# Drain's tables and tokens one step earlier, routing put off by a call, and the next layer's keys and values in the last rounds

## The chip, the cores and the metric

The kernel runs on one core of one Trainium2 chip. The metric is the device time of one execution in microseconds (us). The time of the kernel before is the median of three runs; one further execution was recorded by the hardware profiler, and all lines of the profile come from that one. A core has five engines that run side by side, each with its own instruction order: TensorE (PE; its weight loads are shown as PEld), VectorE (DVE), ScalarE (ACT), GpSimd (POOL) and SyncE (SP, which here issues most transfers). They wait for each other by semaphores.

## The reference

The input is x, 8 sequences of 256 tokens of width 256, and a context of the same shape. Two layers, all in float32, follow each other; each is a gated cross-attention and a gated mixture of experts:

```
x = x + tanh(g_xattn[0]) * attention0(layernorm(x), ctx)     # 16 heads of 16
x = x + tanh(g_ffn[0])   * experts0(layernorm(x))            # 8 experts, the best 2 of each token
x = x + tanh(g_xattn[1]) * attention1(layernorm(x), ctx)     # 16 heads of 16
x = x + tanh(g_ffn[1])   * experts1(layernorm(x))            # 7 experts and a no-op, capacity 256
```

attention: q from layernorm(x), k and v from the context, softmax(q k / 4) v, then an output projection with bias. experts0: logits = x @ gate_w, the two largest, softmax over the two, and for each chosen expert gelu(x W1 + b1) W2 + b2, weighted. experts1: softmax over 8 logits, the top two keep their probabilities; each of the 7 real experts takes the first 256 tokens that chose it, relu(x W1) W2, weighted; tokens that chose the eighth get x times that probability.

## The kernel before, in words

attention(layer) is a software pipeline of steps (b, g), with b from -2 to 7 and g from 0 to 3: b is a batch (a sequence of 256 tokens) and g one of four groups of four heads. The function `step` (L838 to L909) emits one step. The order on TensorE, VectorE, ScalarE and GpSimd is the order in which `step` and its helpers emit instructions (`tc.manual_schedule`, L1070); SyncE's order is left to a scheduler. What is called a drain below is `last_rows` (L1019 to L1065), which follows the last step (7,3).

The parts of a step that matter here:

- `maxima(b+1, g)` (L656, L661): scores of the next batch, and on VectorE their maxima, which `shift` puts into a row of the queries.
- `catch_up` and `some_routing(most, steps)`: the first emits what is in a list of postponed VectorE work and DMAs (`todo`); the second takes up to `most` operations from the routing of finished batches, and stops after `steps` marks ("step") that the routing yields.
- `weigh(b, g)` (L688, L695): scores s of a group, and exponentials ex on ScalarE. `sums(b, g-1)` (L712): weighted sums av of the group before, from ex and the values.
- `divide(b)` at the end of a batch: reciprocals on VectorE, a copy winv on GpSimd (L739), then den and at (L747, L751) on VectorE.
- `output(b-1)` at g=2: the projection po (L761). `normed_rows(b-2)`: the normalised rows rw, on GpSimd (L314), and their DMAs to `normed` and, in layer 0, acc. `turned_rows` (rt, L790) transposes them and `logits` (pl, L802) makes the router's logits.
- `keys(layer, b)` and `values(layer, b)` (pk at L543, pv at L574): keys and values of a batch; they come from the context alone. Each is 8 matmuls, split in two halves around `weigh`. A DMA writes ones into a row of the keys (kT<-ones, L563).

Routing works on groups of batches (0 to 2, 3 and 4, 5, 6, 7). For each group a generator `assign` emits top2, the mask and its running count, two matmuls pp (L367, L368) that give each token its place, the row numbers and idx (L481), and then one indirect DMA of GpSimd for each 128 tokens and each of two choices (the puts, who<-tok,idx, L486), which write a token's number into the list `who` at its place.

In layer 0 the experts' work is a list of tiles of 256 rows, sorted by expert. A table says of each tile which expert it has and where its list begins. The first three tiles (NFIRST = 3) are taken from the first five batches (NKNOWN = 5), so that they can start before the routing is over. `find_firsts` (L913), called at step (7,2), finishes the routing known so far, computes the table (`tables_first`, L1153), and lets SyncE load the first tile's weights (w_in_tf, w_out_tf, b1f, b2f), the token lists (ixf, L1192) and the weights of the other two. In the drain, after `divide(7)`, `gather_firsts` (L934) gathers the tiles' rows by indirect DMA (xrf, L1200), and `work_firsts` works the tiles between the rest of the drain: tf (transposes, L958), hf, gelu, yf.

After layer 0's experts `next_keys` (L1383) computes keys and values of layer 1's b=0 and b=1. Layer 1 starts with loading x_sb from acc (L1081); its step (-1,3) holds keys and values of b=2.

Of the kernel before, what the change touches and what calls it, by code (L numbers as in the profile page):

```python
# [55 lines left out]
def flamingo_kernel(  # L56
# [301 lines left out]
    def count(t0, n, mask):  # L358
        for t in range(n):
            nc.vector.tensor_add(run[:, t0 + t + 1, :], run[:, t0 + t, :], mask[:, t, :])  # L360
            yield
        yield "step"
# [8 lines left out]
    def assign(layer, t0, n, psum, tanh=False):  # L371
# [12 lines left out]
        if layer == 0:  # L384
# [3 lines left out]
            e2 = one("e2")  # L388
            if tanh:
                nc.scalar.activation(e2, d, AF.Tanh, scale=0.5)  # L390
            else:
                nc.scalar.activation(e2, d, AF.Exp)
            mask = per("mask")
            nc.vector.tensor_add(mask, oh1, oh2)
            yield
            yield from count(t0, n, mask)
# [12 lines left out]
        else:  # L409
# [3 lines left out]
            yield  # L413
            nc.scalar.activation(ex, ex, AF.Exp)
            yield "step"
# [35 lines left out]
        if layer == 1:  # L451
            yield from count(t0, n, mask)
            pp = before(layer, t0, n, mask, psum)
            yield "step"
# [130 lines left out]
    def attention(layer):  # L585
# [3 lines left out]
        with ExitStack() as st:  # L589
# [237 lines left out]
            def some_routing(most, steps=99):  # L827

                while most > 0 and groups:
                    got = next(groups[0], "done")  # L830
                    most -= 1
                    if got == "done":
                        groups.pop(0)
                    elif got == "step":
                        steps -= 1
                        if steps == 0:
                            break
# [7 lines left out]
            def step(b, g):  # L845
# [8 lines left out]
                some_routing(9 if b < B - 1 else 18, 1 if b < B - 1 else 3)  # L854
                if g == 0 and 0 <= b - 1:
                    sums(b - 1, NG - 1)
                    divide(b - 1)
                if g > 0 and 0 <= b < B:
                    sums(b, g - 1)
# [9 lines left out]
                if g == 0 and first_new <= b + 2 < B:  # L869
                    work = keys(layer, b + 2, bank, todo)  # L870
# [24 lines left out]
                if 0 <= b < B:  # L895
# [17 lines left out]
            def find_firsts():  # L913
                while groups:
                    some_routing(99)
                pt = ps_s.tile([P, 2 * S], F32, tag="s", name="pfirst")
                tables_first(pt[:, 0:E])
                b1 = small.tile([P, NFIRST, NF], F32, tag="b1f", name="b1f", bufs=1)
                b2row = const.tile([P, NFIRST, D], F32, tag="zrow", name="b2f")
                where = [tile_of(j) for j in range(NFIRST)]  # L920
                known = list(puts[0])
                for j in range(NFIRST):
                    firsts.append(
                        [load_tile(where[j][0], f"f{j}", b1[:, j, :], b2row[:, j, :])]
                    )
                    if j == 0:
                        for i in range(NFIRST):
                            ix = small.tile(
                                [P, 2], I32, tag="ixf", name=f"ixf_{i}", bufs=NFIRST
                            )  # L930
                            load_tokens(0, where[i][1], ix, known)
                            ixs.append(ix)

            ixs = []  # L934

            def gather_firsts():
                for j, ix in enumerate(ixs):
                    xr = sbe.tile([P, 2, W], F32, tag="ex", name=f"xrf_{j}")
                    gather_rows(0, ix, xr, NKNOWN * S)
                    firsts[j] += [ix, xr]  # L940

            def weigh_firsts():
                for j, t in enumerate(firsts):
                    w = small.tile([P, 2], F32, tag="wf", name=f"wf_{j}", bufs=NFIRST)
                    row_weights(w, t[2], r8[:, j : j + 1])
                    t.append(w)

            def work_firsts():
# [5 lines left out]
                def turn(j):  # L954
                    pt = bank(f"tf_{j}")
                    for c in range(NC_):
                        for i in range(2):
                            nc.tensor.transpose(  # L958
                                pt[:, c, ds(i * P, P)], firsts[j][2][:, i, ds(c * P, P)], ident
# [7 lines left out]
                for j in range(NFIRST):  # L967
                    wa, wb, b1, _ = firsts[j][0]
# [22 lines left out]
                    w = firsts[j][3]  # L991
                    firsts[j].append(y)
# [11 lines left out]
            def add_firsts():  # L1004
                for j, ((_, _, _, b2row), ix, _, w, y) in enumerate(firsts):
                    base = sbe.tile([P, 2, D], F32, tag="ex", name=f"basef_{j}")
                    for i in range(2):
                        nc.gpsimd.tensor_scalar(
                            base[:, i, :], b2row, w[:, i : i + 1], None, ALU.mult
# [7 lines left out]
            def last_rows():  # L1017
# [50 lines left out]
            first_new = 3 if layer else 0  # L1068
# [168 lines left out]
    def run_experts(layer):  # L1237
# [9 lines left out]
        with ExitStack() as st:  # L1247
# [135 lines left out]
            def next_keys():  # L1383

                todo = []
                bank = lambda name: ps.tile([P, NC_, S], F32, tag="h", name=name, bufs=3)
                for b in range(2):
                    for work in (keys(1, b, bank, todo), values(1, b, bank)):
                        for _ in work:
                            pass  # L1390
                for f in todo:
                    f()

# [5 lines left out]
            with order():  # L1399
# [3 lines left out]
                if layer == 0:  # L1403
                    next_keys()
# [75 lines left out]
```

## Time and profile before

| | |
|---|---|
| time, median of 3 runs | 964.3 us (960.97 to 979.55) |
| profiled execution | 1003.87 us, span 1002.1 us, mean granted TensorE clock 0.881 |
| TensorE busy | 860.0 us, 86% of the span |
| VectorE, ScalarE, GpSimd busy | 434.7, 318.4, 306.2 us |
| layer 0: attention, drain with the first three tiles, other tiles | 0 to 265, to 342, to 571 us |
| next_keys and the start of layer 1 | 571 to 617 us |
| layer 1: attention, drain, experts | 617 to 825, to 882, to 993 us |

A line of a timeline reads: start and length in us, engine, line of the kernel, operation, output<-input, and a count; in brackets how long the engine stood idle before it and what ended that. A line of the windows reads: the stretch, for each of TensorE, its weight loads, VectorE, ScalarE and GpSimd the busy time and the number of instructions, then TensorE's granted clock (1.00 is full), the busy share of the DMA engines, and GB/s. In the page's second part the span is cut into 40 slices; a digit is a share in tenths. "issue" as what ended an idle time means that the profile shows nothing that the engine waited for.

### The profile page before, as it was taken

How to read it: one execution, taken by the hardware profiler on the slowest of the kernel's cores; microseconds unless marked ns; L12 is line 12 of the kernel's file. 1: busy time of each engine (PE TensorE's matmuls, PEld its weight loads, DVE VectorE, ACT ScalarE, POOL GpSimd, SP SyncE). 2: the span in 40 equal slices, each digit the busy share in tenths (PEclk: the TensorE clock that was granted, in tenths of full speed). 3: DMA queues.
4: the chain of work that ended last, by engine and by line, in shares of the span. 5: the costliest groups of instructions: out<-in, count | busy, mean ns of one | idle time of the engine just before them, and what ended most of it. 6: DMA issues, size and time to landing. Idle time of an engine off the chain costs nothing. (4 is left out here: it accounts for less than half of the span.)

```text
span 1002.1 us, 15457 instructions
## 1 busy us (share of the span) xinstructions
PE 860.0 (86%) x5742; PEld 635.9 (63%) x5742; DVE 434.7 (43%) x1342; ACT 318.4 (32%) x732; POOL 306.2 (31%) x313
## 2 busy tenths in 40 slices
PE   1889999997578999999999958999999984069994
PEld 1556666564267788888888835566665533058883
DVE  1457877675535021111111245477787536501110
ACT  1135555543222232222222123355544351111110
POOL 2011332144334654333333301122221242532432
PEclk9879999896778999999999967599998775579998
DMA  9214442011562858685976281000000011135520
GB/s 267 82 45 123 122 115 60 13 39 38 169 201 66 270 135 234 199 254 163 264 197 188 23 287 58 1 4 23 13 13 3 22 60 51 34 95 163 185 84 32
DMA packets 103438, 110.15 MB, mean 110 GB/s; under 512 B 21888, under 2 KB 91117, under 8 KB 103361
## 3 DMA queue, kind: packets, MB, share of 16 engines
q1 hardware_dynamic: 71360, 80.33, 25.2%
q0 software_dynamic: 11168, 18.32, 7.9%
q10 hardware_dynamic: 20832, 10.50, 3.9%
q8 instruction: 46, 0.75, 0.3%
q14 instruction: 32, 0.25, 0.1%
HBM read 80.21 MB, written 29.55 MB: 110 GB/s over the span
## 5 line engine op out<-in xcount | busy, mean ns | idle before, releaser
L661 DVE TENSOR_REDUCE nm<-s 128x2 f32<-128x512 f32 x256 | 158.9, 684 | 104.3 <-PE s L656 99.6
L695 ACT ACTIVATE ex<-s 128x512 f32<-128x512 f32 x256 | 132.4, 602 | 157.8 <-PE s L688 156.2
L1299 PE MATMUL h<-xg,w_in_t 128*128 128x256 f32 (+1 forms) x576 | 111.1, 351 | 5.0 <-issue 3.3
L1287 DVE COPY xg<-xgt 128x512 f32<-128x512 f32 (+1 forms) x25 | 15.9, 638 | 225.3 <-PE xgt L1283 207.5
L656 PE MATMUL s<-kT,qT 16*128 16x256 f32 x1024 | 108.5, 450 | 5.4 <-ACT ex L695 4.3
L1337 PE MATMUL y<-w_out_t,hT 128*128 128x256 f32 x496 | 111.8, 379 | 0.0
L1299 PEld LDWEIGHTS h<-xg,w_in_t 128*128 128x128 f32 x576 | 97.2, 190 | 17.0 <-issue 4.2
L1309 ACT ACTIVATE hT<-h,b_t 128x256 f32<-128x256 f32 (+1 forms) x144 | 55.1, 442 | 163.9 <-issue 105.9
L1337 PEld LDWEIGHTS y<-w_out_t,hT 128*128 128x128 f32 x496 | 92.9, 190 | 11.9
L712 PE MATMUL av<-ex,va 128*32 128x256 f32 x1024 | 94.0, 437 | 4.9 <-ACT ex L695 2.5
L656 PEld LDWEIGHTS s<-kT,qT 16*128 16x128 f32 x1024 | 69.8, 206 | 37.7 <-issue 10.8
L688 PE MATMUL s<-qT,kT 17*128 17x256 f32 x1024 | 88.4, 437 | 4.4 <-issue 2.7
L486 POOL DMA_INDIRECT who<-tok,idx x64 | 63.2, 987 | 82.8 <-DVE s L504 22.5
L314 POOL TENSOR_SCALAR xn<-x_sb,mv,rstd 128x256 f32<-128x256 f32 x24 | 29.2, 1224 | 186.8 <-DVE rstd L296 136.0
L688 PEld LDWEIGHTS s<-qT,kT 17*128 17x128 f32 x1024 | 55.1, 202 | 32.0 <-issue 26.6
L1200 POOL DMA_INDIRECT xr<-xn,ix x45 | 44.6, 991 | 96.3 <-DMA ix<-who 57.3
L1230 POOL DMA_INDIRECT acc<-ysb,ix x31 | 49.3, 1591 | 74.1 <-DVE ysb L1345 58.8
L712 PEld LDWEIGHTS av<-ex,va 128*32 128x32 f32 x1024 | 33.3, 118 | 52.3 <-issue 24.7
L739 POOL COPY winv<-inv 128x512 f32<-128x512 f32 x16 | 9.9, 621 | 165.5 <-DVE h L294 147.5
L1345 DVE SCALAR_TENSOR_TENSOR ysb<-y,w,base 128x256 f32<-128x256 f32 x45 | 20.0, 479 | 78.6 <-PE y L1337 65.3
L1299 PE MATMUL h<-xg,w_in_b 128*128 128x256 f32 x224 | 52.1, 393 | 1.7 <-DVE w L1224 0.9
L1337 PE MATMUL y<-w_out_b,hT 128*128 128x256 f32 x224 | 50.2, 379 | 0.0
(203 smaller groups left out, 1112.4 us busy)
## 6 DMA issues: line engine op xcount, KB each, us to landing
w_in_t<-in_w_dram SPq DMA_DIRECT2D x18, 1024.0 KB
w_out_t<-in_w_dram SPq DMA_DIRECT2D x18, 1024.0 KB
who<-nobody ACTq DMA_DIRECT2D x14, 512.0 KB
w_in_b<-in_wi_dram SPq DMA_DIRECT2D x7, 1024.0 KB
w_out_b<-in_wx_dram SPq DMA_DIRECT2D x7, 1024.0 KB
xn<-rw SPq DMA_DIRECT2D x16, 256.0 KB
w_in_tf<-in_w_dram SPq DMA_DIRECT2D x3, 1024.0 KB
w_out_tf<-in_w_dram SPq DMA_DIRECT2D x3, 1024.0 KB
```

What stands on the lines that cost most here:

```text
L314: eng.tensor_scalar(dst, x_sb[:, t, :], mv[:, t, 0:1], rstd[:, t : t + 1], ALU.subtract, ALU.mult)
L486: put = nc.gpsimd.indirect_dma_start(out=who[layer][:, :], out_offset=bass.IndirectOffsetOnAxis(ap=idx[:, k, t : t + 1], axis=0), in_=tok[ ...
L656: nc.tensor.matmul(ps[j][:, i, :], qT[r, u, c, ds(i * P, P)], kT[r, u, c, :], start=True, stop=True,)
L661: nc.vector.tensor_reduce(nms[b][:, :, 4 * g + j], ps[j], AX.X, ALU.max, negate=True)
L688: nc.tensor.matmul(ps[j][:, k, :], kT[r, u, c, ds(k * P, P)], qT[r, u, c, :], start=True, stop=True,)
L695: nc.scalar.activation(ex, ps[j], AF.Exp, scale=HD**-0.5)
L712: nc.tensor.matmul(pav[ds(32 * j, 32), u, :], va[:, k, 4 * c + j, ds(32 * u, 32)], exs[j][:, k, :], start=(k == 0), stop=(k == 1),)
L1200: nc.gpsimd.indirect_dma_start(out=xr[:, i, :], out_offset=None, in_=normed[layer][0:among, :], in_offset=bass.IndirectOffsetOnAxis(ap=ix[ ...
L1230: put = nc.gpsimd.indirect_dma_start(out=acc[:, :], out_offset=bass.IndirectOffsetOnAxis(ap=to, axis=0), in_=y, in_offset=None, compute_op ...
L1299: nc.tensor.matmul(ph[:, fi, :], wa[:, c, ds((m * f2 + fi) * P, P)], xg[:, c, 0 : n * P], start=(c == 0), stop=(c == NC_ - 1),)
L1309: nc.scalar.activation(hT[:, f, 0 : n * P], ph[:, fi, :], AF.Gelu, bias=b1[:, f : f + 1],).ins
L1337: nc.tensor.matmul(py[:, i, :], hT[:, f, ds(i * P, P)], wb[:, f, :], start=(f == 0), stop=(f == NF - 1),)
```

## The change

1. Marks that routing yields become "stop" where ScalarE or TensorE work of the routing comes next (after `count`, and around the exponential of layer 1); `some_routing` ends its call there, so that this work is emitted one call later. The small activation e2 comes after the count.
2. In the last round (b = 7) of both layers `some_routing` may take 30 operations and 9 marks instead of 18 and 3, and `weigh(7, g)` comes before `sums(7, g-1)` and not after it.
3. `find_firsts` is split. The table and the first tile's weights come at step (7,1), the token lists at (7,2), and the weights of tiles 1 and 2 after the first tile's gathers, in the drain.
4. Keys and values of layer 1's b=0 and b=1 are computed in layer 0's rounds 6 and 7 (keys at g=0, values at g=3), and `next_keys` is gone. Those of b=2 come in layer 1's steps (0,0) and (0,3) and no longer in (-1,3).

```diff
     def count(t0, n, mask):
...
-        yield "step"
+        yield "stop"
...
+            mask = per("mask")
+            nc.vector.tensor_add(mask, oh1, oh2)
+            yield
+            yield from count(t0, n, mask)
             if tanh:
                 nc.scalar.activation(e2, d, AF.Tanh, scale=0.5)
             else:
                 nc.scalar.activation(e2, d, AF.Exp)
-            mask = per("mask")
-            nc.vector.tensor_add(mask, oh1, oh2)
-            yield
-            yield from count(t0, n, mask)
             pp = before(layer, t0, n, mask, psum)
...
             nc.vector.tensor_tensor(ex, logits, wide(m1), ALU.subtract)
-            yield
+            yield "stop"
             nc.scalar.activation(ex, ex, AF.Exp)
-            yield "step"
+            yield "stop"
...
             pp = before(layer, t0, n, mask, psum)
-            yield "step"
+            yield "stop"
...
+                    elif got == "stop":
+                        break
                     elif got == "step":
...
-                some_routing(9 if b < B - 1 else 18, 1 if b < B - 1 else 3)
+                some_routing(9 if b < B - 1 else 30, 1 if b < B - 1 else 9)
                 if g == 0 and 0 <= b - 1:
                     sums(b - 1, NG - 1)
                     divide(b - 1)
+                if b == B - 1:
+                    weigh(b, g)
                 if g > 0 and 0 <= b < B:
                     sums(b, g - 1)
...
-                if g == 0 and first_new <= b + 2 < B:
-                    work = keys(layer, b + 2, bank, todo)
+                if g == 0 and first_new <= b + 2 < known:
+                    work = keys(layer + (b + 2) // B, (b + 2) % B, bank, todo)
...
-                if g == 3 and first_new <= b + 2 < B:
-                    work = values(layer, b + 2, bank)
-                if layer == 1 and b == -1 and g == 3:
-                    work = itertools.chain(
-                        keys(1, 2, bank, todo),
-                        values(1, 2, lambda name: ps_s.tile([P, 2, D], F32, tag="s", name=name)),
-                    )
+                if g == 3 and first_new <= b + 2 < known:
+                    work = values(layer + (b + 2) // B, (b + 2) % B, bank)
...
-                if 0 <= b < B:
+                if 0 <= b < B - 1:
                     weigh(b, g)
...
+                if layer == 0 and b == B - 1 and g == 1:
+                    find_firsts()
                 if layer == 0 and b == B - 1 and g == 2:
-                    find_firsts()
+                    assert not groups
+                    token_firsts()
...
             def find_firsts():
-                while groups:
-                    some_routing(99)
                 pt = ps_s.tile([P, 2 * S], F32, tag="s", name="pfirst")
                 tables_first(pt[:, 0:E])
...
+                where.extend(tile_of(j) for j in range(NFIRST))
+                load_first(0)
...
+            def load_first(j, gets=()):
+                b1 = small.tile([P, NF], F32, tag="b1f", name=f"b1f_{j}", bufs=NFIRST)
+                firsts.append(load_tile(where[j][0], f"f{j}", b1, b2fs[:, j, :], gets))
...
+            def token_firsts():
                 known = list(puts[0])
...
+                for i in range(NFIRST):
+                    ix = small.tile([P, 2], I32, tag="ixf", name=f"ixf_{i}", bufs=NFIRST)
+                    load_tokens(0, where[i][1], ix, known)
+                    ixs.append(ix)
...
             def gather_firsts():
                 for j, ix in enumerate(ixs):
                     xr = sbe.tile([P, 2, W], F32, tag="ex", name=f"xrf_{j}")
-                    gather_rows(0, ix, xr, NKNOWN * S)
-                    firsts[j] += [ix, xr]
+                    gets = gather_rows(0, ix, xr, NKNOWN * S)
+                    xrs.append(xr)
+                    if j == 0:
+                        for i in range(1, NFIRST):
+                            load_first(i, gets if i == 1 else ())
...
                 sums(B - 1, NG - 1)
                 divide(B - 1)
                 if layer == 0:
+                    gather_firsts()
+                    some_routing(1)
                     nc.scalar.preload_act_table(AF.Gelu)
-                    gather_firsts()
...
-            first_new = 3 if layer else 0
+            first_new, known = (2, B) if layer else (0, B + 2)
...
-            def next_keys():
...
-                if layer == 0:
-                    next_keys()
```

More of the change, by code (lines that the diff above doesn't have):

```diff
@@ L1 @@
-import itertools
 from contextlib import ExitStack
@@ L913, in find_firsts @@
             def find_firsts():
-                while groups:
-                    some_routing(99)
                 pt = ps_s.tile([P, 2 * S], F32, tag="s", name="pfirst")
                 tables_first(pt[:, 0:E])
-                b1 = small.tile([P, NFIRST, NF], F32, tag="b1f", name="b1f", bufs=1)
-                b2row = const.tile([P, NFIRST, D], F32, tag="zrow", name="b2f")
-                where = [tile_of(j) for j in range(NFIRST)]
-                known = list(puts[0])
[L922 to L934, printed above, removed]
+                where.extend(tile_of(j) for j in range(NFIRST))
[3 more added lines that the diff above has]
+                firsts.append(load_tile(where[j][0], f"f{j}", b1, b2fs[:, j, :], gets))
+            where = []
+            if layer == 0:
+                b2fs = const.tile([P, NFIRST, D], F32, tag="zrow", name="b2f")
+            def token_firsts():
+                known = list(puts[0])
+                for i in range(NFIRST):
+                    ix = small.tile([P, 2], I32, tag="ixf", name=f"ixf_{i}", bufs=NFIRST)
+                    load_tokens(0, where[i][1], ix, known)
+                    ixs.append(ix)
+            ixs, xrs, wfs, yfs = [], [], [], []
             def gather_firsts():
@@ L938, in gather_firsts @@
                     xr = sbe.tile([P, 2, W], F32, tag="ex", name=f"xrf_{j}")
-                    gather_rows(0, ix, xr, NKNOWN * S)
-                    firsts[j] += [ix, xr]
+                    gets = gather_rows(0, ix, xr, NKNOWN * S)
[3 more added lines that the diff above has]
+                            load_first(i, gets if i == 1 else ())
             def weigh_firsts():
-                for j, t in enumerate(firsts):
+                for j, xr in enumerate(xrs):
                     w = small.tile([P, 2], F32, tag="wf", name=f"wf_{j}", bufs=NFIRST)
-                    row_weights(w, t[2], r8[:, j : j + 1])
-                    t.append(w)
+                    row_weights(w, xr, r8[:, j : j + 1])
+                    wfs.append(w)
             def work_firsts():
@@ L958, in turn @@
                             nc.tensor.transpose(
-                                pt[:, c, ds(i * P, P)], firsts[j][2][:, i, ds(c * P, P)], ident
+                                pt[:, c, ds(i * P, P)], xrs[j][:, i, ds(c * P, P)], ident
                             )
@@ L967, in work_firsts @@
                 for j in range(NFIRST):
-                    wa, wb, b1, _ = firsts[j][0]
+                    wa, wb, b1, _ = firsts[j]
                     hT = []
@@ L990, in work_firsts @@
                     y = sbe.tile([P, 2, D], F32, tag="ex", name=f"ysbf_{j}")
-                    w = firsts[j][3]
-                    firsts[j].append(y)
+                    w = wfs[j]
+                    yfs.append(y)
                     for i in range(2):
@@ L1004, in add_firsts @@
             def add_firsts():
-                for j, ((_, _, _, b2row), ix, _, w, y) in enumerate(firsts):
+                for j, (ix, w, y) in enumerate(zip(ixs, wfs, yfs)):
                     base = sbe.tile([P, 2, D], F32, tag="ex", name=f"basef_{j}")
@@ L1008, in add_firsts @@
                         nc.gpsimd.tensor_scalar(
-                            base[:, i, :], b2row, w[:, i : i + 1], None, ALU.mult
+                            base[:, i, :], b2fs[:, j, :], w[:, i : i + 1], None, ALU.mult
                         )
@@ L1381, in chain @@
                 second(turns[-1], hT)
-            def next_keys():
[L1385 to L1392, printed above, removed]
             order = lambda: tc.manual_schedule(
```

## The prediction

> **What bounds the kernel now.** I read the page first, then TensorE's timeline around each place the diff touches, then the other queues there. Page, rows 1 and 2:
>
> ```profile
> PE 860.0 (86%) x5742; PEld 635.9 (63%) x5742; DVE 434.7 (43%) x1342; ACT 318.4 (32%) x732; POOL 306.2 (31%) x313
> PE   1889999997578999999999958999999984069994
> PEclk9879999896778999999999967599998775579998
> ```
>
> TensorE is the bound almost everywhere; a slice is 25 us. It is short of work in three places: slices 10 to 13 (the end of layer 0's attention), 23 (the border) and 32 to 35 (the end of layer 1's attention). The change touches all three. The first one, TensorE's timeline:
>
> ```profile
> 261.74 3.38 PE L712 MATMUL av<-ex,va 128*32 128x256 f32 x16 [0.33 <-ACT ex L695]
> 281.36 0.45 PE L958 MATMUL tf<-ident,xrf 128*128 128x128 f32 x1 [16.25 <-DMA xrf<-xn,ixf]
> ```
>
> After the last weighted sums TensorE stands still for 16.25 us, waiting for the first tile's gathered rows. What is behind that, in POOL's and SP's timelines:
>
> ```profile
> 258.36 0.98 POOL L486 DMA_INDIRECT who<-tok,idx  x1 [0.30 <-issue]
> 267.15 0.62 POOL L739 COPY winv<-inv 128x512 f32<-128x512 f32 x1 [7.81 <-DVE h L294]
> 274.98 1.02 POOL L1200 DMA_INDIRECT xrf<-xn,ixf  x1 [7.21 <-DMA ixf<-who]
> 276.31 0.96 POOL L1200 DMA_INDIRECT xrf<-xn,ixf  x1 [0.30 <-issue]
> ```
>
> ```profile
> 263.61 0.42 SPq L1212 DMA_DIRECT2D w_in_tf<-in_w_dram  x1
> 264.22 0.39 SPq L1216 DMA_DIRECT2D w_out_tf<-in_w_dram  x1
> ...
> 266.35 2.19 SPq L1192 DMA_DIRECT2D ixf<-who  x3
> ```
>
> The token list ixf is issued at 266.35, behind 2 MB of weights, and lands at about 274.9, 8.6 us later; POOL then issues two gathers, and their data lands at 281.3. The same kind of load in layer 1 (ix) takes 1.99 us. The weights cannot go earlier because tables_first ends on VectorE at 260.6.
>
> **Layer 0's last round.** (a) Tables go to (7,1) and tokens to (7,2), so weights and ixf both leave before the last sums. What is late next is POOL: its order puts winv(7) before the gathers, and winv(7) starts 2.1 us after the last sums end (265.1 to 267.15) and takes 0.62. Then two gathers (2.3) and their landing (2.2 to 2.5) follow, so the hole is 2.1 + 0.6 + 2.3 + 2.5 = 7.5, say 7.8, against 16.25: **-8.45**. SP carries the rest of the step forward too: table reads, w_in, w_out, b1f, b2f and three ixf; tiles 1 and 2 load only after tile 0's gathers.
>
> (b) Keys and values of layer 1's b=0,1 come into rounds 6 and 7. Their price is the rows where they stood:
>
> ```profile
> 570.91 1.89 PE L543 MATMUL pk<-ctx_sb,wk 128*128 128x256 f32 x8
> ...
> 586.90 1.09 PE L631 MATMUL pt<-ident,xn 128*128 128x128 f32 x4 [8.92 <-DMA x_sb<-acc]
> ```
>
> Start to start 1.73 (pv begins at 572.63, and so on), four of them 6.9 at full clock. At the round's own clock (0.75 in the windows row below) it is 6.9 / 0.75 = **+9.2**. ScalarE's and VectorE's copies of them lie beside it: those engines are busy 13.1 and 21.6 of 40 us.
>
> (c) Scores ahead of sums, and routing's parts put off by a call, remove waits that the timeline shows: 2.60 before pp (L367, waits for mask), 0.65 and 0.33 for ex, and gaps of 0.62, 0.23 and 0.35 that end on issue: **-4.8**. Eight puts stay on POOL, now ahead of gbo(7) (1.25); x_sb with gbo is needed only in the drain, so this costs nothing unless the puts last beyond the last sums.
>
> The clock decides the size of this part. The windows:
>
> ```profile
> 100.00:175.00 75.00, 75.00 (x775) 48.72 (x778) 60.33 (x150) 41.02 (x96) 23.68 (x22) 1.00 0.35 100
> 225.00:265.00 40.00, 33.36 (x212) 18.12 (x212) 21.58 (x91) 13.14 (x30) 17.90 (x18) 0.75 0.17 48
> 265.00:281.00 16.00, 0.12 (x1) 0.00 (x0) 4.10 (x12) 1.76 (x2) 5.42 (x6) 0.61 0.98 336
> 625.00:650.00 25.00, 25.00 (x159) 14.57 (x158) 10.87 (x24) 10.02 (x22) 4.27 (x4) 0.50 0.00 1
> ```
>
> (The second number is TensorE's busy time, the third from the end the clock, then DMA share.) The Trainium skill, "TensorE: Matmul & The Clock Gate", section "What's actually happening", says the array drops to half rate after an idle window of about 3.4 us and comes back after as long a busy one. By the rule the filled round has no such gap and runs at 1.00: keys cost 6.9, and of the 33.4 busy us a quarter goes, 8.3: 6.9 - 4.8 - 8.45 - 8.3 = -14.7. By the rows it stays at 0.75: 9.2 - 4.8 - 8.45 = -4.1. The last row speaks against the rule: fully busy for 25 us, still at 0.50. I stay nearer the rows: **-8**.
>
> A second rule speaks against (a): "DMA: Bandwidth & Descriptors", section "Issuing engines are not separate DMA queues", says that all DMAs end on the same 16 engines and interleave. The row at 265 to 281 agrees (0.98 busy, 336 GB/s, ixf 8.6 instead of 1.99 us). 2.1 MB at 336 GB/s are 6.2 us. If the first tile's weights leave at about 255 they are through at 261, and ixf, which waits for the last put, lands about 264; if they overlap fully ixf lands near 270, about when winv(7) lets POOL go. So between 0 and +2; taken 0.
>
> **The border.** next_keys cost 6.9 us of TensorE but was followed by 8.92 us of waiting for x_sb: hidden. The wait's cause in SP's order:
>
> ```profile
> 574.46 4.03 SPq L563 DMA_DIRECT2D kT<-ones  x2
> 580.42 4.12 SPq L1081 DMA_DIRECT2D x_sb<-acc  x8
> ```
>
> kT<-ones ends its issue at 578.49 and lands about 580.3; it moves away with the keys. Next late is the last add into acc: issued 574.79 + 1.56, landing about 579.05. So **-1.3**, not -6.9.
>
> **Layer 1's start.** pk_2 and pv_2 (608.55 and 610.28, 1.89 each) stood in the shadow of the 2.56 us wait at 608.33 and of a shift; they go to (0,0) and (0,3), where TensorE is full (625 to 650 row). In full shadow before: 2 x 1.73 / 0.50 = 6.9 at most, less the 1.9 that the wait did not cover, so +5; in no shadow 0. Taken **+1.5**, near full clock.
>
> **Layer 1's last round.** This is where the change can hurt. The same larger quota (30 operations, 9 steps instead of 18 and 3) runs here too, and in the built order POOL now issues all twelve who puts of the first group before winv(6) and rw_5. Before, six went ahead and six after:
>
> ```profile
> 803.11 0.63 POOL L739 COPY winv<-inv 128x512 f32<-128x512 f32 x1
> 803.71 2.75 POOL L314 TENSOR_SCALAR rw<-x_sb,mv,rstd 128x256 f32<-128x256 f32 x2
> 806.62 1.08 POOL L486 DMA_INDIRECT who<-tok,idx  x1 [0.17 <-issue]
> ```
>
> ```profile
> 812.93 1.12 PE L790 MATMUL rt<-ident,rw 128*128 128x128 f32 x4
> ```
>
> Puts start 1.28 apart. idx_0 now stands behind lg of pl_4, about 2 us later (797.3): 12 x 1.28 = 15.4, so they end at 812.7, winv at 813.3, rw_5 at 816.1 instead of 806.5. Behind winv wait den and at (VectorE, 0.71 + 0.84) and with them po; behind rw_5 waits rt_5, and behind rt_5 in TensorE's order po, weigh(7,3), sums(7,2), pl_5, pp_6 and sums(7,3). Scores ahead of sums take away ex waits of 3.4 up to here (0.41, 0.87, 0.64, 0.76, 0.36, 0.36), so TensorE is at rt_5 at 809.5 and stands 6.6 us. From rt_5 to the last sums' end was 825.1 - 812.93 = 12.2, less 1.2 of waits is 11: end 827.1, +2 in this profile. In an execution with the full clock the old end would be about 819 (from 800 on at the windows' 0.77 to 0.81 instead of 1.00), the new one 825: +6. In the drain, routing work that is gone from the front lets m_10 start at 842.4 instead of 843.8: -1.4. So +0.6 to +4.6; taken **+3.5**, since the runs, at 961 to 980, were all shorter than the profiled 1003.87.
>
> **Sum.** -8 - 1.3 + 1.5 + 3.5 = -4.3. The profiled execution took 1003.87 us (span 1002.1, clock 0.88), the median of the runs 964.3; it would go to about 999.6. The terms are stalls more than clocked work, so I carry the same difference to the median: **960.0 us**. Own range 951 to 969.
>
> **Rivals.**
> A, the clock comes back: both last rounds become gapless, layer 0 gives the rule's -14.7, and layer 1's puts hide behind TensorE (-1.4, and its ex waits gone, 3.4 and 0.67 and 0.73 after them): -14.7 - 1.3 + 1.5 - 6.2 = -20.7, **944**. For: 100 to 175 at 1.00 with TensorE full. Against: 625 to 650, and twelve puts that exceed what TensorE has to do.
>
> B, slower: POOL's twelve puts. Place: rw_5 and winv(6) ahead of rt_5. Price: rt_5 at 816.1, and after 6.6 us of standing the rest at 0.50 takes 16 and not 11, so 832 against 819: +13, -1.4 from the drain. With layer 0 by the rows (-4.1), -1.3 and +1.5: +7.7, **972**. It decides once the stall and its clock cost more than about 6 us. For: 840 to 882 lies at 0.50 after waits. Against: the wait is only as long as the puts outlast TensorE's work.
>
> C, the change does not do what it says: gathers still wait, behind winv(7) or late puts, and the hole is filled by keys that cost nothing where they were. With the hole at 12 instead of 7.8 layer 0 gives -3.8, and the rest stays (-1.3, +1.5, +3.5): -0.1, **964**. For: POOL's order, which has not changed there.
>
> **How the numbers follow.** Forecast 0.50, A 0.18, B 0.15, C 0.17. 2% is 19.3 us (945.0 and 983.6), about what a measurement of this kernel can tell from no change. Faster by more than that needs most of A: 0.12. Slower needs more than B's price: 0.05. Same: 0.83. The range takes in C, B's and A's near halves: 945 to 975.
>
> **What would show it.** Right: tf_0 waits about 8 us for xrf, with POOL's gathers directly behind winv(7); ixf lands in 2 to 3 us; no wait at pp; four pk/pv groups in rounds 6 and 7; after next_keys' place x_sb<-acc starts about 1.3 us sooner after the last add; in layer 1, twelve puts in a row and a wait of 5 to 8 us at rt_5 for rw. Wrong: rt_5 without a wait (then towards A), tf_0 still over 12 us late (C), or the stretch after rt_5 at 0.50 (B).

## The result, and the profile after

| | before | after |
|---|---|---|
| median (20 runs each) | 969.36 us (960.97 to 983.6) | 961.64 us (956.19 to 964.37) |
| ratio after to before | | 0.9923, 95% interval 0.9905 to 0.994 |
| span and mean granted clock of the profiled execution | 1002.1 us, 0.881 | 958.9 us, 0.899 |

The change made the kernel about 8 us faster, 0.8%. The prediction said 960.0 us from a median of 964.3, within 2% and slightly faster: a difference of -4.3 us, where -7.7 was measured. The time was right; that it came so near was luck in part, since the three runs of before that it started from had a median 5 us under that of the twenty, and since errors in its steps cancelled.

The profile of before that the prediction used came from an execution with long stretches at a reduced clock. So before was profiled a second time (below: "before, second profile", span 968.9 us, clock 0.905), and all comparisons of stages use that one. Rows 1 and 2 of the page of after:

```profile
PE 818.9 (85%) x5742; PEld 616.2 (64%) x5742; DVE 435.4 (45%) x1342; ACT 316.8 (33%) x732; POOL 306.0 (32%) x313
...
PE   2889999999599699999999858999999863089994
...
PEclk9799999999799989999999957999997755589997
```

The work is the same, with as many matmuls as before. The three low places of before are still there, the first one narrower, and the fourteenth slice (312 to 336 us, digit 6) is a new one; it comes back below. TensorE's timelines, cut at the same marks in both kernels, give the stages (us; pt are the transposes of a batch's rows, xgt those of an expert tile's rows):

| stage | before | after | difference |
|---|---|---|---|
| layer 0 attention, to the end of the last sums | 250.5 | 240.3 | -10.2 |
| hole, to tf_0 | 16.7 | 12.1 | -4.6 |
| drain with the first three tiles, to the first xgt | 56.0 | 54.3 | -1.7 |
| layer 0's other tiles, to the last y | 231.1 | 239.9 | **+8.8** |
| border, to layer 1's first pt (keys included before) | 15.7 | 13.1 | -2.6 |
| layer 1 attention, to the end of the last sums | 223.1 | 225.9 | +2.8 |
| layer 1 drain, to its first xgt | 56.9 | 54.6 | -2.3 |
| layer 1 experts | 118.9 | 118.6 | -0.3 |

They sum to -10 us in these two executions. Within attention, a round is the time from one batch's shift (pm, in `shift`) to the next. Of the first row, -4.7 us are the sixth batch's round, -3.0 the two rounds after it up to the last sums, and -2.6 the first steps, where nothing had changed yet: TensorE's clock at 52 to 60 us was 0.50 in before and 0.83 in after, and another kernel with the change was as slow there as before. Over all profiles the second shift, batch 0's, came between 46.6 and 55.0 us, so the start says nothing about the change.

**The hole.** TensorE's, POOL's and SP's timelines of after:

```profile
239.27 1.07 PE L711 MATMUL av<-ex,va 128*32 128x256 f32 x16
242.26 0.51 PE L367 MATMUL pp<-run,ones 128*128 128x16 f32 x2 [1.49 <-DVE run L359]
252.40 0.45 PE L961 MATMUL tf<-ident,xrf 128*128 128x128 f32 x1 [9.63 <-DMA xrf<-xn,ixf]
```

```profile
239.90 0.97 POOL L485 DMA_INDIRECT who<-tok,idx  x1 [0.30 <-issue]
240.87 1.30 POOL L888 TENSOR_TENSOR x_sb<-x_sb,gbo 128x512 f32<-128x512 f32 x1
243.80 0.61 POOL L738 COPY winv<-inv 128x512 f32<-128x512 f32 x1 [1.63 <-DVE inv L735]
248.95 1.02 POOL L1204 DMA_INDIRECT xrf<-xn,ixf  x1 [4.54 <-DMA ixf<-who]
```

```profile
237.22 0.42 SPq L1216 DMA_DIRECT2D w_in_tf<-in_w_dram  x1
237.84 0.39 SPq L1220 DMA_DIRECT2D w_out_tf<-in_w_dram  x1
...
245.84 2.19 SPq L1196 DMA_DIRECT2D ixf<-who  x3
```

winv(7) is done at 244.4, and POOL still waits 4.54 us: not winv but the token list is late. ixf is issued 5 us after the last put ended on POOL (240.87), since the program has it wait for the puts to land, and they land while the first tile's 2 MB of weights are on their way.

**Layer 1's last round.** POOL and TensorE of after:

```profile
767.03 0.97 POOL L485 DMA_INDIRECT who<-tok,idx  x1 [0.30 <-issue]
767.99 0.63 POOL L738 COPY winv<-inv 128x512 f32<-128x512 f32 x1
768.60 2.74 POOL L313 TENSOR_SCALAR rw<-x_sb,mv,rstd 128x256 f32<-128x256 f32 x2
```

```profile
769.87 0.48 PE L789 MATMUL rt<-ident,rw 128*128 128x128 f32 x1 [5.14 <-POOL rw L313]
771.39 0.90 PE L789 MATMUL rt<-ident,rw 128*128 128x128 f32 x3 [1.04 <-POOL rw L313]
```

Twelve puts run without a break from 752.83; then winv; then rw; TensorE stands 6.2 us at rt_5. The windows of after, cut before and behind this wait:

```profile
751.30:764.70 13.40, 12.33 (x98) 6.33 (x98) 3.71 (x22) 9.39 (x21) 9.12 (x10) 0.74 0.18 57
764.70:771.40 6.70, 0.51 (x6) 0.19 (x2) 2.67 (x4) 0.00 (x0) 6.09 (x7) 0.50 0.09 29
771.40:785.70 14.30, 12.99 (x71) 8.58 (x71) 8.51 (x35) 5.48 (x13) 1.17 (x1) 0.62 0.18 55
```

Behind the wait TensorE works at a clock of 0.62 up to the last sums.

**What paid for it.** 4.7 us in layer 0's attention and 6.2 in layer 1's, where the last round hides them, come from a place that the prediction did not look at: the sixth batch's round. In before (second profile), ScalarE and TensorE in layer 1:

```profile
725.27 0.24 ACT L414 ACTIVATE ex<-ex 128x48 f32<-128x48 f32 x1 [6.19 <-DVE ex L412]
725.42 2.04 ACT L695 ACTIVATE ex<-s 128x512 f32<-128x512 f32 x4
```

```profile
726.05 2.14 PE L656 MATMUL s<-kT,qT 16*128 16x256 f32 x12 [1.95 <-ACT ex L695]
728.12 1.93 PE L712 MATMUL av<-ex,va 128*32 128x256 f32 x16
```

Routing's exponential takes 0.24 us, but it stands on ScalarE ahead of the four exponentials of the scores and waits 6.19 us for VectorE. TensorE then stands 1.95 us, and its next groups run slowly: 12 matmuls of s take 2.14 us where 16 take 1.29 at full clock, and 16 of av 1.93 where they take 1.07. The granted clock was 1.00 up to the wait, 0.50 from 728 to 732 us, and 1.00 again from 734. In after the same exponential comes behind the scores' four, and nobody waits:

```profile
710.49 2.06 ACT L694 ACTIVATE ex<-s 128x512 f32<-128x512 f32 x4 [3.35 <-PE s L687]
712.42 0.86 ACT L548 ACTIVATE qT<-pq,bqk 128x256 f32<-128x256 f32 x2
713.35 0.24 ACT L413 ACTIVATE ex<-ex 128x48 f32<-128x48 f32 x1
```

From shift to shift this round took 29.9 us before and 23.7 after in layer 1 (-6.2), and 30.1 before and 25.4 after in layer 0 (-4.7).

**Where it was given back.** In layer 0's other tiles TensorE waits for the third tile's rows. TensorE's timeline of after, then POOL's:

```profile
333.46 0.45 PE L1287 MATMUL xgt<-ident,xr 128*128 128x128 f32 x1 [4.69 <-DMA xr<-xn,ix]
336.59 0.90 PE L1287 MATMUL xgt<-ident,xr 128*128 128x128 f32 x3 [2.69 <-DMA xr<-xn,ix]
```

```profile
320.42 1.63 POOL L1234 DMA_INDIRECT acc<-ysbf,ixf  x1 [6.41 <-issue]
...
330.49 1.02 POOL L1204 DMA_INDIRECT xr<-xn,ix  x1 [0.16 <-issue]
331.82 1.58 POOL L1234 DMA_INDIRECT acc<-ysbf,ixf  x1 [0.30 <-issue]
333.70 1.01 POOL L1204 DMA_INDIRECT xr<-xn,ix  x1 [0.30 <-issue]
```

Before (second profile) had one wait there, and its first gather of the third tile went out behind three adds:

```profile
346.58 0.55 PE L1283 MATMUL xgt<-ident,xr 128*128 128x128 f32 x3 [2.73 <-DMA xr<-xn,ix]
```

```profile
337.99 1.04 POOL L1200 DMA_INDIRECT xr<-xn,ix  x1 [0.16 <-issue]
```

POOL's order in this stage is left to the scheduler. In before the third tile's two gathers (xr) stood behind three and four adds of the first tiles into acc; in after they stand behind five and six. Every kernel that has part 1 of the change, that with part 1 alone too, had its gathers behind two more adds than before, unless an edit below moved them.

### The profile page after: what moved, and what is told of

Its sections match the earlier page's. It is cut to its first block, busy times and chain, and to the rows that moved or that the text cites. A ratio compares the mean times of both kernels' runs of the same rounds, so it can differ in the third digit from the quotient of the medians.

```text
span 958.9 us, 15454 instructions
## 1 busy us (share of the span) xinstructions
PE 818.9 (85%) x5742; PEld 616.2 (64%) x5742; DVE 435.4 (45%) x1342; ACT 316.8 (33%) x732; POOL 306.0 (32%) x313
## 5 line engine op out<-in xcount | busy, mean ns | idle before, releaser
L1341 PE MATMUL y<-w_out_t,hT 128*128 128x256 f32 x496 | 113.8, 384 | 0.0
L655 PE MATMUL s<-kT,qT 16*128 16x256 f32 x1024 | 98.0, 431 | 1.2 <-ACT qT L548 0.6
L687 PE MATMUL s<-qT,kT 17*128 17x256 f32 x1024 | 83.6, 416 | 2.8 <-DMA qT<-nmT 1.4
L655 PEld LDWEIGHTS s<-kT,qT 16*128 16x128 f32 x1024 | 63.3, 197 | 30.4 <-issue 10.4
L711 PE MATMUL av<-ex,va 128*32 128x256 f32 x1024 | 77.3, 415 | 1.1 <-DVE nat L725 1.1
L687 PEld LDWEIGHTS s<-qT,kT 17*128 17x128 f32 x1024 | 53.5, 192 | 27.1 <-issue 19.4
L711 PEld LDWEIGHTS av<-ex,va 128*32 128x32 f32 x1024 | 28.9, 114 | 36.4 <-issue 18.5
```

Of the source, the lines that this page charges most:

```text
L655: nc.tensor.matmul(ps[j][:, i, :], qT[r, u, c, ds(i * P, P)], kT[r, u, c, :], start=True, stop=True,)
L687: nc.tensor.matmul(ps[j][:, k, :], kT[r, u, c, ds(k * P, P)], qT[r, u, c, :], start=True, stop=True,)
L711: nc.tensor.matmul(pav[ds(32 * j, 32), u, :], va[:, k, 4 * c + j, ds(32 * u, 32)], exs[j][:, k, :], start=(k == 0), stop=(k == 1),)
L1341: nc.tensor.matmul(py[:, i, :], hT[:, f, ds(i * P, P)], wb[:, f, :], start=(f == 0), stop=(f == NF - 1),)
```

## The experiments

Every experiment starts from the changed kernel unless said otherwise; ratios are to the kernel before on the same chip (after: 0.9923). The runs were made in four sets, in which before had medians of 969.8, 976.8, 995.3 and 974.8 us (the second and third on the same chip), and after itself was not run in them. So ratios of different sets are compared only roughly, and stages of the profiles are compared first, with the ratio beside them.

**A second profile of before.** No edit.

> The kernel before once more, unchanged, for a profile at the ordinary clock. Expected: span about 960 to 968 us. The hole before tf_0 is the same 16 us whatever the clock (it is made of transfers). In layer 1, rt_5 is not waited for; if the prediction's estimate at full clock holds, layer 1's stretch from its first pt to its first expert transpose (xgt) is 3 to 5 us shorter than the changed kernel's; if the early routing pays in the drain what the puts cost, it is the same or longer.

Measured: 970.71 us, span 968.9. The hole is 16.73 us. Layer 1 from its first pt to its first xgt takes 280.0 us before and 280.5 after: the second case, not the first. That seemed to say that the puts cost nothing in the end; the next run says otherwise.

**Layer 1 at the old quota.**

```diff
-                some_routing(9 if b < B - 1 else 30, 1 if b < B - 1 else 9)
+                most, marks = (30, 9) if layer == 0 else (18, 3)
+                some_routing(9 if b < B - 1 else most, 1 if b < B - 1 else marks)
```

> The changed kernel with layer 1's last round at the old quota (18 operations, 3 marks), layer 0 as changed. Theory (twelve puts in a row hold winv and rw back): six puts go behind rw_5, the waits of 5.14 and 1.04 us at rt_5 go, and the kernel is 3 to 5 us faster than the changed one (about 0.995 of it). Rival (the drain gets back what the puts cost): the routing that is not done early comes behind the last sums on VectorE, the last chain of layer 1 is as late as before, and the time is the same within 1.5 us or longer.

Measured: 952.38 us, 0.9838 (0.9795 to 0.9881). POOL, TensorE and the windows:

```profile
757.02 0.63 POOL L738 COPY winv<-inv 128x512 f32<-128x512 f32 x1
757.62 2.74 POOL L313 TENSOR_SCALAR rw<-x_sb,mv,rstd 128x256 f32<-128x256 f32 x2
760.53 1.07 POOL L485 DMA_INDIRECT who<-tok,idx  x1 [0.17 <-issue]
```

```profile
759.28 1.07 PE L711 MATMUL av<-ex,va 128*32 128x256 f32 x16
760.28 0.69 PE L789 MATMUL rt<-ident,rw 128*128 128x128 f32 x4
```

```profile
760.30:770.40 10.10, 9.13 (x72) 5.78 (x68) 3.12 (x9) 8.17 (x18) 8.24 (x9) 0.76 0.42 139
```

rt_5 follows the sums without a wait. From the last shift to the last sums' end it is 19.8 us, against 34.4 in after and 25.0 in before: the quota alone costs 14.5 us there, and 6.4 come back in the drain (61.0 against 54.6 us); 8.1 remain. (Attention and drain are 9.6 us shorter in all, but 1.7 of that is the round before, which takes 28.8 us in after and 27.1 here, and 27.1 also in two kernels below that keep the large quota; so it is not the quota's.) The theory is confirmed in kind, at about twice the expected size.

The 14.5 us have two parts. rt_5 with all its rows starts 20.1 us after the last shift instead of 9.7: 10.4 us. From there to the last sums it is 14.3 us at a clock of 0.62 instead of 10.1 at 0.76, with one more pair of routing's matmuls (pp): 4.2 us. The wait of 6.2 us is less than the first part because TensorE, at 0.74, came late to rt_5 itself. In three kernels below that keep the twelve puts (keys back, table back, token lists first) TensorE ran at 1.00 up to rt_5 and waited longer; with keys and values back:

```profile
766.35 0.48 PE L789 MATMUL rt<-ident,rw 128*128 128x128 f32 x1 [6.96 <-POOL rw L313]
```

Yet the stretch from the last shift to the last sums was 34.3 to 34.4 us in all of them. So POOL's row of puts sets the time of rt_5, and the clock before it changed nothing.

**Layer 1 with the puts behind winv and rw, large quota kept.**

```diff
                 catch_up()
+                early = layer == 1 and b == B - 1 and g == 0
+                if early:
+                    sums(b - 1, NG - 1)
+                    divide(b - 1)
+                    normed_rows(b - 2, nc.gpsimd)
                 some_routing(9 if b < B - 1 else 30, 1 if b < B - 1 else 9)
```

> The changed kernel with layer 1's step (7,0) in another order: the last sums of b=6, winv and rw_5 come before the routing, so before the twelve puts on GpSimd; the large quota stays. Theory (it is the puts' place ahead of winv and rw that costs, not the early routing): no wait at rt_5, the stretch from the last shift to the last sums goes from 34 us back to about 20 to 22, the drain stays short, and the kernel is 8 to 12 us faster than the changed one, as fast as or faster than with the old quota (950 to 953). Rival (VectorE's burst of early routing delays tr, den and nat, and so TensorE, whatever GpSimd's order): the last round keeps 5 us or more of the 14, and the kernel is slower than with the old quota by 3 us or more.

Measured: 955.5 us, 0.9809 (0.9759 to 0.9858). rt_5 does not wait; from the last shift to the last sums it is 28.7 us instead of 34.4, with the drain still short (54.5). So the order is worth 5.7 of the 8.1 us that the quota costs with its drain. The edit sets it on every engine, not on POOL alone. The rival has the rest: the last round keeps 8.9 of the 14.5 us, where the theory had expected 20 to 22 us for the whole round. TensorE now waits 3.12 us for the scores' exponentials, which stand on ScalarE behind rows of x_sb that wait for VectorE, and 2.92 us at pp for the mask from VectorE.

```profile
757.62 2.56 PE L687 MATMUL s<-qT,kT 17*128 17x256 f32 x12 [3.12 <-ACT ex L694]
```

**Keys and values back behind layer 0's experts** (next_keys restored, known = B for layer 0; b=2 stays).

> The changed kernel with the keys and values of layer 1's b=0 and b=1 computed after layer 0's experts again; those of b=2 stay at (0,0) and (0,3). Theory (moved work costs in the last rounds 4 x 1.73 = 6.9 us of TensorE, and was hidden behind the wait for x_sb): layer 0's last sums come 6 to 7 us earlier, the border costs 1.3 to 2.7 us more, so 4 to 5 us faster than the changed kernel. Rival 1 (the keys fill stalls and keep the clock up): the last round is hardly shorter, and the kernel is 1 to 3 us slower. Rival 2 (the hole is bound by the puts' landing and not by TensorE): the last sums come earlier but tf_0 does not; then the time is 1.3 to 2.7 us longer.

Measured: 956.98 us, 0.9875 (0.9828 to 0.9922). Counted from the same shift at the start, the last sums come 6.1 us earlier; the hole is 1.8 us longer, the border 15.6 instead of 13.1, the other tiles 2.1 shorter. The first part of the theory holds: the keys cost nearly what their matmuls take, 6.1 us of 6.9, and nothing was to be had for them at the border beyond 2.5 us. The second rival has a part, since 1.8 us go back into the hole, where ixf again leaves 5 us after the last put. The 2.1 us of the other tiles were in no theory. By the stages moving the keys was a loss of about 4 us; the ratios of the whole times (0.9875 and 0.9923, with intervals that overlap) do not show it for sure.

**Table, weights and tokens back at (7,2).**

> The changed kernel with the table, the first tile's weights and the token lists at step (7,2) again, and the weights of tiles 1 and 2 issued behind the token lists as before. Theory (the early table is what shortens the hole): the wait before tf_0 goes from 9.6 us back to about 13 to 16 us, +4 to +6 us, ratio to the changed kernel about 1.005. Rival (the puts' landing bounds it and the table comes early enough in any case): the wait stays within 2 us of 9.6, and the time within 2 us.

Measured: 967.55 us, 0.9998 (0.9972 to 1.0024). Last sums to tf_0: 18.6 us instead of 12.1; every other stage is within 1.4 us. So part 3 of the change is worth 6.5 us; table, weights and token lists move together here, and what each of them gives was not separated.

```profile
260.02 0.45 PE L959 MATMUL tf<-ident,xrf 128*128 128x128 f32 x1 [13.87 <-DMA xrf<-xn,ixf]
```

**Token lists ahead of the first tile's weights.**

```diff
-                load_first(0)
 ...
-                    load_tokens(0, where[i][1], ix, known)
+                    gots.append(load_tokens(0, where[i][1], ix, known))
                     ixs.append(ix)
+                load_first(0, gots)
```

> The changed kernel with the first tile's weights behind the token lists (waiting for them) and not ahead of them. Theory (the 2 MB of weights, at 237 to 244 us, hold up the landing of the last puts and of ixf): ixf is issued 2 to 3 us earlier and lands in about 2 us instead of 3, tf_0 comes 3 to 4 us earlier after the last sums, and the kernel is 2 to 4 us faster. Rival (the weights are then late): tf_0 comes earlier but the first hf waits for w_in, time equal or longer.

Measured: 963.85 us, 0.9892 (0.9843 to 0.9942). SP and TensorE:

```profile
242.00 2.19 SPq L1197 DMA_DIRECT2D ixf<-who  x3
...
245.93 0.40 SPq L1218 DMA_DIRECT2D w_in_tf<-in_w_dram  x1
```

```profile
249.04 0.44 PE L962 MATMUL tf<-ident,xrf 128*128 128x128 f32 x1 [6.81 <-DMA xrf<-xn,ixf]
252.95 0.90 PE L962 MATMUL tf<-ident,xrf 128*128 128x128 f32 x3 [3.47 <-DMA xrf<-xn,ixf]
```

With no weights in flight ixf is issued 1.6 us after the last put's end instead of 5.0, and the hole is 9.1 us: the weights did hold up the puts. But now the weights travel beside the gathers, whose second half comes 3.47 us later, and the drain is 3.2 us longer. Nothing is gained.

**Part 1 alone, on the kernel before** (the marks "stop" and the place of e2).

> The kernel before with the first part of the change alone (routing's ScalarE and TensorE parts put off by a call); quotas, tables, scores and keys as before. Theory (in the fifth round routing's small exponential stood on ScalarE ahead of the scores' four, and waited 6.2 us for VectorE; TensorE then stood about 1.9 us and ran at half clock for a while, once in each layer): the sixth shift comes about 6 us earlier after the fifth in layer 0 and in layer 1. The build also gives GpSimd the changed kernel's order of gathers behind layer 0's first tiles, so if that order is what costs the changed kernel about 7 us there, this kernel loses them too: net -5 to -6 us against before (about 963 to 965). Rival (the put-off only moves the same stall into a later round or the drain): the round is shorter, the following ones longer, and the time stays within 2 us of before, or above it by the 7 us of the order.

Measured: 980.87 us, 1.006 (1.002 to 1.0099): slower, by 0.6%. The stages show why. The sixth round is shorter in both layers, as expected (30.1 to 25.5 and 29.9 to 23.7). But what is put off is late elsewhere: layer 0's next round is 4.0 us longer, the hole is 21.1 instead of 16.7, and layer 1's drain 61.4 instead of 56.9. The other tiles take 238.0 instead of 231.1, with GpSimd's gathers in the order of the changed kernel. So the stall is really gone, but the forecast of 963 to 965 was wrong; the rival (shorter round, longer later ones, and the order's price on top) came nearest. Part 1 pays in the changed kernel only together with the parts that take up the routing which it puts off.

```profile
270.02 0.45 PE L960 MATMUL tf<-ident,xrf 128*128 128x128 f32 x1 [21.09 <-DMA xrf<-xn,ixf]
```

**The third tile's weights wait for its gathers.**

> The changed kernel with one added wait: the third tile of layer 0's main expert chain loads its weights only when its own rows are gathered (two gathers waited for), GpSimd's order unchanged. Theory (three tiles' weights, 6 MB, fill the DMA engines just when GpSimd's adds into acc have to land, and the third tile's gathers stand behind these adds in GpSimd's order): the add that stood 6.4 us starts 3 to 5 us earlier, TensorE's waits of 4.69 and 2.69 us for xr shrink to under 3 together, and the kernel is 3 to 6 us faster than the changed one (956 to 958). Rival 1 (the order alone does it, whatever the traffic): waits and time within 1.5 us of the changed kernel's. Rival 2: the weights now come too late, and the wait moves to the third tile's first matmuls; time equal or longer.

Measured: 960.27 us, 0.9851 (0.9802 to 0.9899). POOL, then TensorE:

```profile
311.49 1.63 POOL L1234 DMA_INDIRECT acc<-ysbf,ixf  x1 [1.95 <-issue]
```

```profile
324.24 0.30 PE L1287 MATMUL xgt<-ident,xr 128*128 128x128 f32 x1 [1.61 <-DMA xr<-xn,ix]
327.34 0.55 PE L1287 MATMUL xgt<-ident,xr 128*128 128x128 f32 x3 [2.80 <-DMA xr<-xn,ix]
```

The add waits 1.95 us and not 6.41, so the third tile's weights have a part in that wait. TensorE's two waits fall from 7.4 to 4.4 us, and the other tiles from 239.9 to 237.7. It is a part of the cause, less than expected. The low ratio is not this edit's alone: 2.2 us are 0.2%.

**The bias rows ahead of the adds,** alone and together with the last edit.

> The changed kernel with the first tiles' bias rows (basef, six GpSimd operations) computed ahead of the first add into acc, so that GpSimd's built order has one gather of the third tile (xr_5) one add earlier and no bias row between the add that stood 6.4 us and these gathers. Theory (the gathers stand behind the adds in GpSimd's order, and what lies between them counts): TensorE's waits for xr, 4.69 and 2.69 us in the changed kernel, shrink by 2 to 4 us together, and layer 0's other tiles take 2 to 4 us less than 239.9. Rival (the adds' landing alone sets the gathers): the bias rows are then hidden in the wait anyway, the waits stay, time the same within 1.5 us.

> Both edits: the bias rows ahead of the adds, and the third tile's weights waiting for its gathers. If order and traffic are the two causes of the 8.8 us that layer 0's other tiles took longer than before (239.9 against 231.1), this takes back 5 us or more of them (under 235), against 2.2 for the added wait alone. Rival (something else in that stretch): it takes back no more than 3.

Measured: 958.79 us, 0.9921 (0.9882 to 0.996), and 956.65 us, 0.9911 (0.987 to 0.9951). The third tile's gathers now stand behind four and five adds, one fewer than in after and one more than in before. The other tiles take 236.5 and 234.6 us: -3.4 and -5.3 of the 8.8. So GpSimd's order and the weights' traffic make at least 5.3 of them; the rest was not isolated (before's exact order of GpSimd was not rebuilt). In the whole times these few us are not told apart from after.

**Putting the good parts together** (old quota in layer 1, keys back, third tile's wait; and the same without that wait).

> The changed kernel with three edits together: layer 1's last round at the old quota, keys and values of layer 1's b=0 and b=1 after layer 0's experts again, and the third tile's weights waiting for its gathers. If the three stages add up as their profiles say (-9.6 in layer 1, -4.0 for the keys, -2.2 for the third tile), the span is 16 us under the changed kernel's and the ratio to before about 0.976. If the keys' place and the third tile's wait share one slack, 3 us less of it.

> As the last one without the third tile's added wait. If that wait is worth its 2.2 us here too, this kernel is 2 us slower than the last one; if the order of GpSimd's gathers alone decides, the two are the same within 1 us. Ratio to before about 0.978.

Measured: 0.9767 (0.9713 to 0.982) and 0.9791 (0.9739 to 0.9842), as expected. These are the best ratios of all, about 1.5% under the changed kernel's, but their intervals overlap with those of the old quota alone and of the other order, and the two are not told apart from each other. In that set every kernel was slower (before 995.33 us, these two 972.05 and 972.08), so their times cannot be set beside the others.

The stages do not bear out the sum behind the expectation. Layer 1's attention and drain take 279.0 and 277.1 us, not the 270.9 of the old quota alone, and layer 0's last two rounds 60.8 and 57.7 us, where the kernel with the keys back alone took 38.8. That kernel has the same code there as the second of these two. So it is not shown that the gains add up. The third tile's wait can be seen in its stage: 235.0 against 239.4 us.

One thing shows better here than anywhere else. The last sums come so late that the token lists are there in time, and the gathers follow winv(7) at once (the kernel without the wait, POOL and TensorE):

```profile
256.38 1.02 POOL L1205 DMA_INDIRECT xrf<-xn,ixf  x1 [0.38 <-issue]
```

```profile
259.89 0.45 PE L962 MATMUL tf<-ident,xrf 128*128 128x128 f32 x1 [5.15 <-DMA xrf<-xn,ixf]
```

The hole is 7.0 and 7.1 us in these two profiles, close to the 7.8 of the prediction.

## Why the prediction was right or wrong

The time (960.0 against 961.64) and the class were right. The steps, in us, by the second profile of before and that of after:

| term | predicted | measured |
|---|---|---|
| layer 0: the hole | -8.45 | -4.6 |
| layer 0: last two rounds (keys, waits, clock) | +0.45, what the taken -8 leaves | -3.0 |
| border | -1.3 | -2.6 |
| layer 1: start | +1.5 | -1.7 |
| layer 1: last two rounds and drain | +3.5 | +8.5 |
| sum of these | -4.3 | -3.4 |
| sixth batch's round, both layers | 0 | -10.9 |
| layer 0's other tiles | 0 | +8.8 |
| start, drain of layer 0, layer 1's experts | 0 | -4.6 |

- **Layer 0's hole** was taken as 7.8 us and measures 12.1. The failed step is "between 0 and +2; taken 0" for the DMA engines: the weights left at 237.2, only 3 us before the last sums ended, where the prediction had them leave 10 us before (255 against 265.1); the puts landed beside them, and ixf came last instead of winv(7). Without POOL's wait of 4.54 us for ixf the hole would be about 7.6, and it was 7.0 and 7.1 where ixf came in time. The rule that the prediction named against the change (the Trainium skill, "DMA: Bandwidth & Descriptors", section "Issuing engines are not separate DMA queues") had the right side: taking the weights out of the way gave 3.0 us (9.1 against 12.1). Part 3 paid 6.5 us by the experiment, against 8.45 predicted.
- **Keys in the last rounds** were taken at +6.9 to +9.2 us. The experiment gives 6.1 in layer 0's rounds: right, at the full-clock end. Their old place was hidden, as predicted, and the border gained 2.6, not 1.3.
- **Waits and clock in these rounds** gave more than they were taken for. Without the keys (the experiment) the two rounds take 38.8 us against 47.8 before, -9.0; the prediction had -4.8 for waits, and for the clock what is left between -8 and the other terms. The places were in part wrong: the gaps of 0.62, 0.23 and 0.35 that ended on "issue" are not in the second profile of before, and the 2.60 before pp is 0.27 there. The av groups of the last round took 2.1 to 3.4 us in it and four of five take 1.07 in after, where the scores come ahead of the sums; that part of the change was not tried alone.
- **The clock weighing** (-14.7 by the rule, -4.1 by the rows, taken -8): layer 0 up to tf_0 gave -14.8, but not for the reason weighed. Of it 4.7 us are the sixth round and 2.6 the start; what is left, about -7.5, is near -8 only because the hole gave less and the rounds more than the sum had. Nor did the rule hold as the prediction cites it (the Trainium skill, "TensorE: Matmul & The Clock Gate", section "What's actually happening"): a wait of 1.95 us, well under its idle window of about 3.4 us, was followed by a clock of 0.50.
- **Part 1 of the change was not priced outside the last round.** This is the largest error. The page's group "PE s L656 ... 5.4 <-ACT ex L695 4.3" had shown a wait for ex in the first scores, and no line of the prediction asked where it was. It was worth 6.2 us in layer 1 and 4.7 in layer 0.
- **Layer 1's start** was taken at +1.5 and gained 1.7. In before pk_2 and pv_2 took 3.62 and 2.81 us, because they ran in the cold stretch after a wait; at (0,0) and (0,3) a part of them runs at full clock. The prediction took the clock of (0,0) from a profile in which it was 0.50.
- **Layer 1's puts** were right in mechanism: twelve in a row, then winv, then rw, and a wait of 6.2 us at rt_5 against 6.6 predicted. The price was too small. Rival B's sum, with the clock, said +13 against the undisturbed round; the old quota shows 14.5. In the kernel as a whole it was covered by part 1, which is why the time did not show it.
- **The drain** of layer 1 gained 2.3 us, 1.4 predicted; it stands in the row of layer 1's last rounds.
- **Layer 0's other tiles** (+8.8) were in no case and no rival: a change of GpSimd's order in a stage that the diff does not touch.

So two sums of about 10 us that were not seen, part 1's gain and the loss behind the first tiles, nearly cancelled each other. Rival C had the hole's size (12 us) and, with its "late puts", the cause, and the prediction's own sign for it (tf_0 over 12 us late) came true, just. The prediction gives two ranges, 951 to 969 and 945 to 975; the measured time lies in both.

## What to carry to other kernels

When a small operation with a late input stands on an in-order engine ahead of urgent work, price the wait in every round in which it occurs, not only in the round that the diff names, and add the reduced clock that follows. A larger quota for postponed work needs a look at what is queued behind it on the engine that executes its last part, here GpSimd. After any change in a stage, compare the order of the engines that are left to a scheduler in the next stage as well.

## What the runs showed of the hardware

A wait of 1.95 us in a stretch at full clock was followed by a granted clock of 0.50 for at least 4 us (728 to 732 us in the second profile of before), and the round was 6.2 us longer than without the wait. After the waits of 5.14 and 1.04 us at rt_5 the clock was 0.62 over 14.3 us, with TensorE busy 13.0 of them; the kernel without these waits had 0.76 over nearly the same work. The last of GpSimd's small indirect writes were waited for 1.6 us after their issue had ended with no weights in flight, and 5.0 us while 2 MB of weights were (ixf, issued at 242.00 after 240.44, and at 245.84 after 240.87). In the profile of the kernel with the old quota and the keys back, ScalarE stood 10.95 us and VectorE 6.11 us before 223.5 us, at places where the profile names no wait of the program (it calls what ended them "remote"); what causes such gaps was not tried.
